# Two graph layers on one core: last norms shared with GpSimd, and weight, score and norm places of layer 1's u stages moved

## The chip, the cores and the metric

The kernel runs on 1 core of one Trainium2 chip. A core has five engines that run their own instruction streams side by side: PE (TensorE, matrix products into PSUM), DVE (VectorE), ACT (ScalarE), POOL (GpSimd) and SP (SyncE, which here only issues DMAs). The metric is device microseconds (us) of one execution; less is better.

## The reference, cut to what matters

For each of two layers, with `N` = 2048 nodes, a batch of 8 and 64 features:

```python
x_g = jnp.einsum('knm,bmc->bnkc', supports, x)        # each node gathers over the graph
w   = jnp.einsum('nd,dkio->nkio', embedding, weight)  # a weight matrix for each node
out = jnp.einsum('bnki,nkio->bno', x_g, w) + bias
x   = _layernorm(x + out, axis=-1)                    # over the 64 features
```

Layer 0 has the supports I, A and 2A²−I. Layer 1 has these and one more, the row softmax of relu(E Eᵀ), where E are the node embeddings (2048 x 16). `_layernorm` subtracts the mean over the 64 features and divides by the square root of the variance plus 1e-5.

## The kernel before, in words

The work is 40 stages of about 30 to 45 us each, five phases of eight blocks of 256 nodes: A0 and B0 are layer 0, A1, Z1 and V1 are layer 1. Stage n is block n % 8 of phase n // 8.

- **A1** (stages 16 to 23, the "u stages" of layer 1) makes u = A x for a block. Stage 16 is a plain product (`straight`, line 484). The others use seven half-size products instead of eight (`strassen`, line 504), with sums of operands that DVE makes ahead.
- **Z1** (stages 24 to 31) makes the softmax support times x. Stage 24 is plain. Stage 25 is called "narrow": its numerators are made by halves, during stage 24.
- **V1** (stages 32 to 39) makes A u. Stage 39 is the last one, and what follows it is the tail.

Each stage has a second job, for the block of the stage before: PE makes the per-node weights (`weights`, line 336: embedding times weight pool, into PSUM tiles `pw`), ACT and DVE copy them to SBUF (`w<-pw`: of three tiles in a job ACT takes the first and the third and DVE the second), PE multiplies them with the features (`apply`, line 370, PSUM tile `po`), and DVE adds what belongs to each node into `acc` under a mask (four instructions of 128x256 for each `apply`). For the last phase of a layer, `post` (line 399) normalizes `acc` in three parts: part 0 makes the mean, subtracts it and has ACT square the result; part 1 sums the squares and has ACT take the root; part 2 makes the reciprocal, multiplies and stores. For layer 1 in the tail the store goes to SP's queue.

The order of instructions on an engine is program order, and it is written by hand. `put(n, place, f)` plans f into stage n. A generator, `product`, issues the stage's matmuls and counts them; whenever the count reaches a place, the planned calls are issued between two matmuls. A stage is 64 counts long if its product is plain and 56 otherwise, and a place is scaled by length/64, so that place 16 in a 56-count stage means "after 14". Every engine takes its instructions in this order, so a call that waits on an engine holds up all that stands behind it there.

Three shared resources matter. Three PSUM tiles (`big`) go around between weights, scores, transposes, bias and `apply`; two further banks hold the accumulators of the products. The weight pools come in four chunks of 8 pairs for a block (512 KB each) through three buffers `wst`; when a job has used up a chunk, its buffer is refilled by a DMA from SP's queue. The jobs of a u stage cover the pairs 0-6, 6-12, 12-18, 18-24, 24-28 and 28-32, so the second job frees chunk 0's buffer, and chunk 3, which that buffer receives, is first used by the fifth job.

For the softmax, `scores_of_rows` (line 733) makes the scores of 128 rows in two halves (PE tile `pr`; DVE applies the relu and takes the row's maximum), and `statistics` (line 745) has ACT make two exponentials of 128x1024 with their sums. `numerators` and `normalize` (line 722, two DVE multiplications of 128x1024 per call in the narrow stage) make the softmax itself.

Of the kernel before, what the change touches and what calls it, by code (L numbers as in the profile page):

```python
# [15 lines left out]
P = 128  # L16
# [32 lines left out]
def two_graph_layers(ctx: ExitStack, tc: tile.TileContext, x, x_t, adj_b, adj_q, layers, out):  # L49
# [231 lines left out]
    class Stage:  # L281
# [114 lines left out]
                    dve.scalar_tensor_tensor(acc, src, mask[:, i:i + 1], acc, op0=ALU.mult, op1=ALU.add)  # L396


        def post(self, part, s0=0, s1=GROUPS):
            a = self.acc[:, s0:s1, :]  # L400
            flat = a.rearrange("p s o -> p (s o)")
            g = s1 - s0
            if self.kk == 0:
                if part == 0:
                    pool.dma_start(out=pd[self.li, self.j], in_=flat)
                return
            if part == 0:
                mean = small.tile([P, GROUPS], F32, tag="mean", name="mean")[:, 0:g]
                dve.tensor_reduce(mean, a, AX.X, ALU.add)
                dve.tensor_scalar(mean, mean, 1.0 / C, None, op0=ALU.mult)  # L410
                dve.tensor_tensor(a, a, mean[:, :, None].to_broadcast([P, g, C]), op=ALU.subtract)
                if self.sq is None:
                    self.sq = one.tile([P, GROUPS, C], F32, tag="sq", name="sq")
                act.activation(self.sq[:, s0:s1, :].rearrange("p s o -> p (s o)"), flat, AF.Square)
            elif part == 1:
                dev = small.tile([P, GROUPS], F32, tag="dev", name="dev")[:, 0:g]
                dve.tensor_reduce(dev, self.sq[:, s0:s1, :], AX.X, ALU.add)
                act.activation(dev, dev, AF.Sqrt, bias=eps, scale=1.0 / C)
                self.dev[s0] = dev
            else:  # L420
                rstd = small.tile([P, GROUPS], F32, tag="rstd", name="rstd")[:, 0:g]
                dve.reciprocal(rstd, self.dev[s0])
                dve.tensor_tensor(a, a, rstd[:, :, None].to_broadcast([P, g, C]), op=ALU.mult)
                if self.li == 1:
                    rows = slice(self.j * NB * B + s0 * P, self.j * NB * B + s1 * P)
                    (pool if s1 - s0 == GROUPS else sp).dma_start(out=rows_of(out[rows, :]), in_=a)
                    return
                pool.dma_start(out=rows_of(x1d[self.j][s0 * P:s1 * P, :]), in_=a)
# [55 lines left out]
        def straight(self, right):  # L484
            accs = [self.accumulator("pu") for _ in range(SB)]
            for m0 in range(0, NJ, 4):
                self.a = adj.next().rearrange("p (m n) -> p m n", n=NB)
                pairs = [(s, m) for s in range(SB) for m in range(m0, m0 + 4)]
                if self.n == 0 and m0 < NJ - 4:
                    pairs.sort(key=lambda at: at[1])  # L490
                for s, m in pairs:
                    pe.matmul(accs[s], self.a[:, m - m0, s * P:(s + 1) * P], right[m],
                              start=(m == 0), stop=(m == NJ - 1))
                    yield 2
                    if m == NJ - 1:
                        copy(s if self.n else 1, self.slabs[s], accs[s])
            self.store_u()

        def store_u(self):
# [4 lines left out]
        def strassen(self, right):  # L504
# [45 lines left out]
            def add(dst, a, b, op=ALU.add):  # L550

                if not isinstance(dst, tuple):
                    dve.tensor_tensor(dst, a, b, op=op)
                elif self.kk == 0:
                    dve.tensor_tensor(self.slabs[dst[0]][:, dst[1] * half:(dst[1] + 1) * half], a, b, op=op)
                else:
                    if self.wide:
                        to = self.pair[dst[0]].features()[64:128, :, :]
                    else:
                        r = 64 if self.narrow else 0  # L560
                        to = self.features()[r:r + 64, dst[0] * P:(dst[0] + 1) * P, :]
                    for par in range(2):
                        of = lambda x: x[64 * par:64 * par + 64, :].rearrange("p (q n) -> p n q", n=nodes)
                        dve.tensor_tensor(to[:, :, 4 * dst[1] + par:4 * dst[1] + par + 3:2], of(a), of(b), op=op)

            c00, c01, c10, c11 = (0, 0), (0, 1), (1, 0), (1, 1)
            w1, w4, v = temps[:3]
# [281 lines left out]
    for n, st in enumerate(stages):  # L849
# [11 lines left out]
        if phase == "A0":  # L861
            for c in range(NJ // 4 if st.j == 1 else 0):
                put(n, 16 * c + 10, st.sums_of_a, c)
            if sevens:
                place_weights(n + 1, (1, 5, 14, 23, 32))
                turned, bursts, posts = 34.5, (39.5, 39.5, 39.5, 39.5), (51,)
            else:
                spread(n + 1, 1, 31, weights)
                turned, bursts, posts = 33, (38, 38, 38, 38), (50,)
        elif phase == "B0":  # L870
            for c in range(NJ // 4 if st.j == 0 else 0):
                put(n, (10, 26, 36, 57)[c], st.sums_of_a, c)
            if st.j == 7:
                spread(n, 35, 54, weights)
                bursts, posts = (0, 0, 6, 10), ()
                put(n + 1, 16, st.load_x, range(SB))
                for k in range(6):
                    put(n + 1, (11 if k < 3 else 12.5) + 0.5 * k, st.post, k % 3, 8 - k // 3 * 8, 16 - k // 3 * 8)
            else:
                spread(n + 1, 3, 13, weights)  # L880
                bursts, posts = (19, 19, 29, 29), (38, 46.5, 50)
                put(n + 2, 5, st.load_x, range(SB))
        elif phase == "A1":
            if sevens:
                place_weights(n + 1, (1, 12.5, 17, 22.3, 31.3))
            else:
                spread(n + 1, 12, 34.5, weights)
            turned, bursts, posts = 4, (43, 43, 43, 43), (56,)
            for s, h, place in ((0, 0, 38), (0, 1, 40), (1, 0, 57), (1, 1, 60)):
                put(*((n, place) if st.j or s == 0 else (n + 1, place - 43)), st.scores_of_rows, s, h)  # L890
            put(n, 41, st.statistics, 0)
            put(*((n, 62) if st.j else (n + 1, 19)), st.statistics, 1)
            put(n + 1, 24, st.store_c)
        elif phase == "V1":
            if st.j:
                put(n, 4, *weights.pop(0))
            spread(n, (22 if 0 < st.j < 7 else 12 if st.j else 4), (62 if st.j < 7 else 42), weights)
            bursts, posts = (4, 4, 4, 4), (15, 19, 23)
            put(n, 20, st.load_z)
# [18 lines left out]
        elif st.narrow:  # L918
            put(24, 1, st.take_halves)
            put(23, 48, st.load_e)  # L920
            for t, places in enumerate(((3, 7, 22), (37, 39.5, 57))):
                for i, place in enumerate(places):
                    put(24, place, *((st.numerators, t, i) if i < 2 else (st.normalize, t)))
            put(26, 10, load_last_phase)
        elif st.wide:
            first, even, odd = (n - 2, (16, 24, 32), (40, 48, 56)) if n % 2 == 0 else (n - 2, (28, 36, 44), (4, 12, 20))
            load = ((25, 40) if n == 28 else (n - 3, 4)) if n % 2 == 0 else (n - 3, 10)
            if n == 26:
                first, even, odd, load = 25, (4, 12, 18), (22, 30, 36), (24, 40)
            elif n == 27:  # L930
                first, even, odd, load = 25, (66, 69, 72), (44, 52, 58), (25, 8)
            put(*load, st.load_e)
            for t, places in enumerate((even, odd)):
                for i, place in enumerate(places):
                    at = (first, place) if place < 64 else (first + 1, place - 64)
                    put(*at, *((st.numerators, t, i) if i < 2 else (st.normalize, t)))
        else:
            st.p = [None] * 8
            for c in range(8):
                if c < 3:  # L940
                    put(n - 1, (50, 54, 62)[c], st.scores, c)
                else:
                    put(n, 8 * (c - 2), st.scores, c)

    last = stages[-1]
    for c in (2, 3):
        put(len(stages) - 1, 50, last.apply, c)
    put(len(stages) - 1, 58, last.post, 0, 8, 16)
    for n, st in enumerate(stages):
        done = 0  # L950
        todo = sorted(plans[n])
# [10 lines left out]
        done = 1000  # L962
        catch_up()
    last.post(1, 8, 16)
    last.post(2, 8, 16)
    last.apply(0)
    last.post(0, 0, 4)
    last.apply(1)
    for part, g0, g1 in ((0, 4, 8), (1, 0, 4), (2, 0, 4), (1, 4, 8), (2, 4, 8)):
        last.post(part, g0, g1)  # L970


# [44 lines left out]
```

## Time and profile before

| | |
|---|---|
| median of 3 runs | 1467.26 us (1466.7 to 1468.25) |
| the profiled execution's own time | 1467.24 us |
| its span, first to last instruction | 1465.5 us |
| PE busy | 1438.7 us, 98% of the span |
| DVE busy | 972.9 us, 66% |
| ACT busy | 485.4 us, 33% |
| POOL busy | 204.5 us, 14%, of which most is issuing DMAs |
| chain that ended last | PE 92%, DVE 3%, DMA 3%, issue 1%, ACT 1% |

The span leaves out 1.7 us of the execution's own time. "PE" is the matmuls and "PEld" the weight loads that overlap them. In a timeline the columns are start, duration, engine, line and operation, output and inputs with shapes, how many were merged, and in brackets the idle time before and who ended it. All instructions carry line 43, that of a helper, so they are told apart by their tiles. Matmul ends are modelled, and each fp32 matmul of the program shows as two records.

### The profile page before, as it was taken

To read this page: it belongs to the slowest core of one execution; us is meant where nothing else is said; L and a number is where in the kernel's file an instruction comes from. 1 tells how busy PE (TensorE), PEld (TensorE's weight loads), DVE (VectorE), ACT (ScalarE), POOL (GpSimd) and SP (SyncE) were. 2 spreads that over 40 slices of the span, in tenths; PEclk is the share of its full clock that TensorE was granted. 3 is DMA by queue.
4 is the path that set the end of the run, shared out by engine and by line. 5 is a ranking of instruction groups with operands and counts; after the bars stand their busy time and mean duration, and the time that the engine had idled before them with its cause. 6 is when DMAs were issued, how large, how long until landed. Compare 5 with 4: busy or idle time off the path is not lost.

```text
span 1465.5 us, 31573 instructions
## 1 busy us (share of the span) xinstructions
PE 1438.7 (98%) x13502; PEld 1185.3 (81%) x13502; DVE 972.9 (66%) x1648; ACT 485.4 (33%) x640; POOL 204.5 (14%) x339
## 2 busy tenths in 40 slices
PE   9999999999999999999999999999999999999996
PEld 4577777778999998577777777799888988888885
DVE  3866666648766666865566666689794566666666
ACT  1444444432212113255444444612110233333232
POOL 5212222110111111211011111011000000000000
PEclk9999999999999999999999999999999999999999
DMA  9888888885666666478787877323314766666662
GB/s 363 279 260 273 293 289 276 277 307 187 197 206 202 204 202 210 150 171 204 183 207 164 199 212 177 43 79 95 83 47 115 248 182 198 193 187 195 191 190 58
DMA packets 88379, 285.50 MB, mean 195 GB/s; under 512 B 14000, under 2 KB 19632, under 8 KB 86640
## 3 DMA queue, kind: packets, MB, share of 16 engines
q1 hardware_dynamic: 55568, 175.13, 40.6%
q0 software_dynamic: 27200, 94.71, 21.9%
q10 hardware_dynamic: 5472, 13.63, 2.8%
q8 instruction: 107, 1.75, 0.5%
q14 instruction: 32, 0.26, 0.1%
HBM read 217.33 MB, written 62.41 MB: 191 GB/s over the span
## 4 chain that ended last, share of the span: by engine, by line
PE 92%; DVE 3%; DMA 3%; issue 1%; ACT 1%; ACTq 0%; DVEq 0%
PE pa L43 67%; PE po L43 14%; PE pw L43 8%; DMA wst<-wd 2%; PE pt L43 1%; PE ps L43 1%; PE pr L43 1%; DMA x<-in_x 1%; DVE acc L43 1%; DVE u L43 1%; DVE mean L43 0%; ACT w L43 0%; DVE w L43 0%; DVE t L43 0%; DVE dev L43 0%
## 5 line engine op out<-in xcount | busy, mean ns | idle before, releaser
L43 ACT ACTIVATE w<-pw 128x1024 f32<-128x1024 f32 x309 | 304.6, 1029 | 403.7 <-PE pw L43 402.5
L43 DVE SCALAR_TENSOR_TENSOR acc<-po,mask,acc 128x256 f32<-128x256 f32 (+1 forms) x640 | 247.0, 426 | 67.3 <-PE po L43 54.5
L43 DVE COPY w<-pw 128x1024 f32<-128x1024 f32 x127 | 155.4, 1224 | 199.6 <-PE pw L43 199.3
L43 PE MATMUL pa<-a,u 128*128 128x128 f32 (+1 forms) x2048 | 264.1, 285 | 2.8 <-issue 2.8
L43 PEld LDWEIGHTS pa<-a,u 128*128 128x128 f32 x2048 | 245.0, 192 | 15.4 <-issue 5.4
L43 PE MATMUL pa<-x,a 128*128 128x256 f32 (+1 forms) x816 | 239.3, 435 | 0.8 <-DMA x<-in_x 0.5
L43 PE MATMUL po<-w,t 128*32 128x256 f32 (+1 forms) x5120 | 206.2, 337 | 5.9 <-issue 4.8
L43 PE MATMUL pa<-u,a 128*128 128x256 f32 x832 | 202.7, 387 | 0.0
L43 PEld LDWEIGHTS pa<-x,a 128*128 128x128 f32 x816 | 149.6, 190 | 61.2 <-issue 37.6
L43 PEld LDWEIGHTS po<-w,t 128*32 128x32 f32 (+1 forms) x5120 | 128.6, 108 | 77.4 <-issue 13.2
L43 PEld LDWEIGHTS pa<-u,a 128*128 128x128 f32 x832 | 151.9, 190 | 28.9 <-issue 5.4
L43 PE MATMUL pw<-e,wst 64*128 64x256 f32 x1680 | 144.7, 295 | 4.3 <-ACT w L43 1.7
L43 PEld LDWEIGHTS pw<-e,wst 64*128 64x128 f32 x1680 | 111.9, 184 | 36.2 <-ACT w L43 11.9
L43 PE MATMUL pa<-a,x 128*128 128x128 f32 x768 | 93.0, 277 | 0.0
L43 PEld LDWEIGHTS pa<-a,x 128*128 128x128 f32 x768 | 88.3, 192 | 2.4
L43 PE MATMUL pa<-w,u 128*128 128x256 f32 x384 | 85.8, 379 | 0.0
L43 PE MATMUL pa<-a,w 128*128 128x128 f32 x672 | 81.3, 277 | 0.0
L43 PEld LDWEIGHTS pa<-w,u 128*128 128x128 f32 x384 | 72.0, 190 | 9.3
L43 PEld LDWEIGHTS pa<-a,w 128*128 128x128 f32 x672 | 77.3, 192 | 2.5 <-issue 1.4
L43 ACT ACTIVATE t<-pt 64x512 f32<-64x512 f32 x64 | 40.6, 635 | 76.5 <-DVE t L43 64.2
L43 ACT ACTIVATE sq<-acc 128x1024 f32<-128x1024 f32 (+2 forms) x19 | 17.5, 922 | 145.1 <-DVE acc L43 135.2
L43 POOL DMA_DIRECT2D e<-ed x80 | 42.1, 531 | 167.5 <-PE pw L43 144.8
(127 smaller groups left out, 1306.2 us busy)
## 6 DMA issues: line engine op xcount, KB each, us to landing
wst<-wd SPq DMA_DIRECT2D x108, 512.0 KB, 6.3
a<-in_adj_q SPq DMA_DIRECT2D x90, 512.0 KB, 5.3
a<-sd SPq DMA_DIRECT2D x88, 512.0 KB, 4.4
sd<-a POOLq DMA_DIRECT2D x24, 512.0 KB, 4.5
bx<-bx POOLq DMA_DIRECT2D x32, 256.0 KB, 5.6
acc<-bx POOLq DMA_DIRECT2D x16, 512.0 KB, 6.7
pd<-acc POOLq DMA_DIRECT2D x16, 512.0 KB, 4.6
acc<-pd POOLq DMA_DIRECT2D x16, 512.0 KB, 8.7
```

What stands on the lines that cost most here:

```text
L43: return self._tc.keep_in_program_order(f(*args, **kwargs))
```

## The change

1. **Tail.** `post` gets an argument that names the engine of its two large elementwise operations (subtract the mean, multiply by the reciprocal). In the last stage the groups 8 to 16 and 0 to 4 give both to POOL; the groups 4 to 8 keep them on DVE. The parts are put in another order. The last four DVE additions before the last `apply` calls are cut by halves of nodes (two instructions of 64x256 become four of 64x128), so that the first 64 nodes are complete earlier. The first two `apply` calls of the last stage stand two matmuls earlier.
2. **u stages 18 to 23.** The six weight jobs of the block before stand at other places: after 11, 14, 18, 23, 28 and 32 matmuls instead of 11, 15, 19, 23, 27 and 31. In stages 17 and 24 they stay where they were.
3. **Stage 17.** The second half of the last scores of block 0 stands two matmuls later, and its statistics with it (after the second weight job, before the third, as before).
4. **Stage 16.** The copy of the second half of u from PSUM moves from ACT to DVE, ahead of a DVE sum of 128x2048.
5. **Stage 24.** The first `normalize` of the narrow stage moves from place 22 to 47.5, behind the 16 masked additions; the second from 57 to 51, with no DVE instruction between its old place and its new one.

No transfer is added or taken away, and the order of DMA issues on SP, ACT and POOL stays.

```diff
-        def post(self, part, s0=0, s1=GROUPS):
+        def post(self, part, s0=0, s1=GROUPS, by=dve):
...
-                dve.tensor_tensor(a, a, mean[:, :, None].to_broadcast([P, g, C]), op=ALU.subtract)
+                by.tensor_tensor(a, a, mean[:, :, None].to_broadcast([P, g, C]), op=ALU.subtract)
...
-                dve.tensor_tensor(a, a, rstd[:, :, None].to_broadcast([P, g, C]), op=ALU.mult)
+                by.tensor_tensor(a, a, rstd[:, :, None].to_broadcast([P, g, C]), op=ALU.mult)
...
-                        copy(s if self.n else 1, self.slabs[s], accs[s])
+                        copy(s if self.li == 0 and self.n else 1 - self.li, self.slabs[s], accs[s])
...
-                    for par in range(2):
-                        of = lambda x: x[64 * par:64 * par + 64, :].rearrange("p (q n) -> p n q", n=nodes)
-                        dve.tensor_tensor(to[:, :, 4 * dst[1] + par:4 * dst[1] + par + 3:2], of(a), of(b), op=op)
+                    parts = 2 if self.n == len(stages) - 1 and dst == c01 else 1
+                    for some in range(parts):
+                        at = slice(some * nodes // parts, (some + 1) * nodes // parts)
+                        for par in range(2):
+                            of = lambda x: x[64 * par:64 * par + 64, :].rearrange("p (q n) -> p n q", n=nodes)[:, at, :]
+                            dve.tensor_tensor(to[:, at, 4 * dst[1] + par:4 * dst[1] + par + 3:2], of(a), of(b), op=op)
...
-            if sevens:
-                place_weights(n + 1, (1, 12.5, 17, 22.3, 31.3))
-            else:
-                spread(n + 1, 12, 34.5, weights)
+            place_weights(n + 1, (12, 15.5, 20.5, 25.5, 32, 36) if 0 < st.j < 7 else (12, 16.5, 21, 25.5, 30, 34.5))
...
-            for s, h, place in ((0, 0, 38), (0, 1, 40), (1, 0, 57), (1, 1, 60)):
-                put(*((n, place) if st.j or s == 0 else (n + 1, place - 43)), st.scores_of_rows, s, h)
+            for s, h, place, later in ((0, 0, 38, 0), (0, 1, 40, 0), (1, 0, 57, 14.2), (1, 1, 60, 19)):
+                put(*((n, place) if st.j or s == 0 else (n + 1, later)), st.scores_of_rows, s, h)
...
-            put(*((n, 62) if st.j else (n + 1, 19)), st.statistics, 1)
+            put(*((n, 62) if st.j else (n + 1, 20)), st.statistics, 1)
...
-            for t, places in enumerate(((3, 7, 22), (37, 39.5, 57))):
+            for t, places in enumerate(((3, 7, 47.5), (37, 39.5, 51))):
...
-        put(len(stages) - 1, 50, last.apply, c)
-    put(len(stages) - 1, 58, last.post, 0, 8, 16)
+        put(len(stages) - 1, 49, last.apply, c)
+    put(len(stages) - 1, 58, last.post, 0, 8, 16, pool)
...
     last.post(1, 8, 16)
-    last.post(2, 8, 16)
+    last.post(2, 8, 16, pool)
     last.apply(0)
-    last.post(0, 0, 4)
+    last.post(0, 0, 4, pool)
     last.apply(1)
-    for part, g0, g1 in ((0, 4, 8), (1, 0, 4), (2, 0, 4), (1, 4, 8), (2, 4, 8)):
-        last.post(part, g0, g1)
+    last.post(0, 4, 8)
+    last.post(1, 0, 4)
+    last.post(1, 4, 8)
+    last.post(2, 0, 4, pool)
+    last.post(2, 4, 8)
```

## The prediction

> **What bounds the kernel now.** I read the page's chain first: 92% of what ended last is PE, and PE is 98% busy. So a change is worth only what it takes from PE's idle time, or from the tail, where PE has finished. Next, PE's waits from stage 16 to 24 (us in total, times, longest):
>
> ```profile
> PE pw L43 <- ACT w L43: 1.7, 3, 1.1
> PE pw L43 <- DMA wst<-wd: 1.5, 3, 0.6
> PE pt L43 <- ACT u L43: 1.0, 1, 1.0
> PE pw L43 <- DVE p L43: 1.0, 1, 1.0
> PE pr L43 <- ACT w L43: 0.5, 1, 0.5
> ```
>
> That is 5.7 us in all, and the edits touch all of it but the longest ACT wait (1.1, stage 24). Third, the timeline of two of these places. Stage 18, a chunk's DMA and the job that waits for it:
>
> ```profile
> 675.36 0.32 SPq L43 DMA_DIRECT2D wst<-wd  x1
> ...
> 684.00 0.74 PE L43 MATMUL pw<-e,wst 64*128 64x256 f32 x8 [0.61 <-DMA wst<-wd]
> ```
>
> Stage 24, where two multiplications of `normalize` stand ahead of what frees a PSUM tile:
>
> ```profile
> 934.23 2.35 DVE L43 TENSOR_TENSOR p<-p,c 128x1024 f32<-128x1024 f32 x2
> 935.80 0.73 PE L43 MATMUL pw<-e,wst 64*128 64x256 f32 x8
> 936.77 0.67 DVE L43 SCALAR_TENSOR_TENSOR p<-ps,c 128x512 f32<-128x512 f32 x1
> 937.49 0.51 PE L43 MATMUL pw<-e,wst 64*128 64x256 f32 x4 [0.96 <-DVE p L43]
> ```
>
> Fourth, the tail. From 1450.66 on DVE works nearly without a gap:
>
> ```profile
> 1450.66 0.86 DVE L43 TENSOR_TENSOR t<-pa,temps 64x256 f32<-64x256 f32 x2 [0.85 <-PE pa L43]
> 1451.55 0.69 DVE L43 TENSOR_REDUCE dev<-sq 128x8 f32<-128x512 f32 x1
> 1453.58 2.04 DVE L43 SCALAR_TENSOR_TENSOR acc<-po,mask,acc 128x256 f32<-128x256 f32 x4
> 1456.32 0.42 DVE L43 TENSOR_TENSOR acc<-acc,mean 128x256 f32<-128x256 f32 x1
> 1456.66 2.04 DVE L43 SCALAR_TENSOR_TENSOR acc<-po,mask,acc 128x256 f32<-128x256 f32 x4
> 1460.72 0.42 DVE L43 TENSOR_TENSOR acc<-acc,rstd 128x256 f32<-128x256 f32 x1
> 1461.90 0.18 DVE L43 RECIPROCAL rstd<-dev 128x4 f32<-128x4 f32 x1 [0.42 <-ACT dev L43]
> 1462.11 0.42 DVE L43 TENSOR_TENSOR acc<-acc,rstd 128x256 f32<-128x256 f32 x1
> ```
>
> The last store is issued at 1462.56, and the span ends at 1465.5. Whatever makes DVE's chain shorter ends the kernel sooner, one to one.
>
> **What the Trainium skill says.** "GPSIMD Engine Reference", § 3.1, gives 4497 ns for a two-input fp32 elementwise operation of 2048 elements on GpSimd: 2.2 ns an element. No run here shows one: POOL's computing so far is memsets and a mask. § 2.1 of that page adds that the first call to a freshly loaded routine pays about 6 us; not shown here either. "SBUF — State Buffer", § SBUF: two separate sides: a GpSimd operation and a DVE operation with two SBUF inputs exclude each other for a whole instruction. DVE's masked additions take one input from PSUM, so they should pass freely.
>
> **u stages 18 to 23.** The time from one `po` to the next in the chain is 42.07, 42.01, 41.52, 41.54, 41.38 and 41.76 us. The fifth has no DMA wait; over it the others lose 0.69, 0.63, 0.14, 0.16 and 0.38, in all 2.0, of which 1.48 is listed (0.61, 0.55, 0.32). A matmul of the program takes 0.48 us here (1.92 for 4). The second job comes one matmul sooner, so chunk 0's buffer is free, and SP issues chunk 3's load, 0.48 us sooner (674.88 for 675.36). The fifth job comes one matmul later: without a wait at 683.87 instead of 683.39. Landing before: about 683.95. So 0.96 us of room stand against at most 0.69 of wait. I do not count on an earlier landing: the DMA rate is about 400 GB/s from 679.5 to 685, three loads share it, and the third starts earlier too (third job at 677.17 for 677.65). With the old landing 0.08 stays in stage 18, 0.02 in stage 19. Moved along: each job issues 8 to 12 matmuls, two copies on ACT or one, and one on DVE. The second job's third tile needs ACT's copy that ends at 674.48; PE gets there at 674.95. Behind the sixth job, half a microsecond later, `pr` and `pb` need its tiles 0.2 to 0.4 us after they are free, and DVE's relu comes 0.14 later, against its idle 0.35 before the masked additions. SP's order is the same. Gain: 1.9; bounds 0.4 (new tile waits in each stage) and 2.0.
>
> **Stage 24.** Without the two multiplications (2.35 us) DVE reaches `p<-ps` when `ps` is there, about 935.1, and is done at 935.8, before PE wants the tile at 936.4. A job of 12 takes 0.91, so PE goes on at 936.70 instead of 937.93. Gain: 1.1; bounds 0.8 and 1.2. The multiplications go behind the masked additions, which end at 958.48: four now, 4.70 us to 963.2. The next DVE instruction, `t<-pa`, starts at 963.27 because PE is not ready earlier. The cover is just enough; if it were gone, each 0.1 us late would be 0.1 on PE only if `t<-pa` (1.4 us, to 964.67) ran past 966.9, where stage 25 takes the bank. So nothing.
>
> **Stages 16 and 17.** PE waits 1.01 at 623.81 for ACT's copy, which starts at 623.16 behind other ACT work, after PE's 622.81. On DVE it can start at about 622.95 and takes 0.68 (the other half's row): PE at 623.65, a gain of 0.15. The sum of 2.28 us behind it ends at 625.9; DVE's next copy starts at 628.64. In stage 17 the later scores take away the wait of 0.50, but they start at 633.02 instead of 632.77, so relu, maximum and ACT's two exponentials are 0.25 later, and ACT's copies of the third job, at 637.60 now, come at 637.85. The fourth job waits for these (0.17 and 0.40 now). PE leaves it 0.25 later, whatever it gained before. Sum: a loss of 0.1, between −0.3 and +0.5.
>
> **Tail.** Step by step, with POOL estimated from the page's price and a start: 1.25 us for 512 elements, 0.7 for 256.
> - `apply` two matmuls sooner: its additions end at 1446.9, not 1447.4. POOL's first subtraction 1448.8 to 1450.1, ACT's square to 1450.85. DVE needs it at 1451.8, so 1.0 us to spare.
> - Additions by halves: 0.43 for 256 elements and, from 0.70 for 512, 1.04 ns an element and 0.155 fixed; 0.29 each for 128. Two done at 1451.24, so PE starts at 1451.31 (−0.27) and the additions start at 1453.31. All four end at 1451.82, the reduction at 1452.55, the reciprocal at 1453.1: in time, since the multiplication of 0.69 is POOL's.
> - Additions to 1455.35, mean to 1456.01; POOL subtracts to 1456.8, ACT squares to 1457.3. Second additions to 1458.08 (they saved 0.27 and 0.34), mean, subtraction and square to 1459.67. DVE's two reductions end at 1459.53 and 1460.11, ACT's roots at 1459.97 and 1460.46.
> - POOL multiplies from 1460.4 to 1461.1, and SP stores. DVE's reciprocal ends at 1460.68; its multiplication, with two SBUF inputs, would end at 1461.13 alone, 1461.55 if it waits for POOL's. Before, 1462.53. SP needs 0.37 to 0.39 for an issue, and the last stands behind POOL's store: about 1461.6 against 1462.56.
>
> Gain: 1.0. Bounds: 1.4 with POOL as fast as DVE's 0.42 and no exclusion; a loss where POOL is slow (rival 3).
>
> **Sum.** −1.9 −1.1 +0.1 −1.0 = −3.9. Of the profiled execution's 1467.24 that leaves 1463.3 (span 1461.6); the median, 1467.26, is the same to 0.02.
>
> **Rivals.**
> 1. The tail gives nothing: POOL takes 0.9 us more for each operation, or the store on SP waits. For: the price is from a page, not a trace. Against: DVE's chain is visibly the bound and loses 1.5 us of work. 1464.3, and 1465 at worst.
> 2. Chunk 3 lands as late as its new job, or tiles become the wait: the jobs' gap of 2.35 us is less than the 2.83 now, with ACT's copies taking 1.94. u stages give 0.4: 1464.8. Against: 0.4 us to spare, worked out above; the stage without a DMA wait has no other.
> 3. Slower: POOL's start. If each POOL operation takes e longer than estimated, the first has 1.0 us to spare, the second subtraction 1.9, and the last multiplication none: the tail loses (e−1.0)+(e−1.9)+e. At e = 2.3 it eats the whole 3.9; at 3.3 the kernel is 3.2 slower, 1470.4. A single 6 us at the first operation costs 5: 1468.3. Against: POOL's memset of 128x2048 takes 1.82 in this profile, its mask 0.31.
>
> **How the numbers follow.** A measurement of this kernel tells about 0.2%, 2.9 us, from no change. As worked out: 0.64 (1462.4 to 1464.2, all faster). Rival 1: 0.15, half of it on each side of 1464.3. Rival 2: 0.13, same. Rival 3: 0.05, of which 0.02 is within the bound. Something unseen, slower: 0.03. Faster 0.64 + 0.07 = 0.71; same 0.08 + 0.13 + 0.02 = 0.23; slower 0.06. The range 1462.4 to 1465.2 takes in rivals 1 and 2 nearly whole.
>
> **What would show it.** Right: no `wst` wait of PE in stages 18, 19 and 23, and `po` to `po` at 41.4; no DVE wait near 936; DVE's multiplications, four in a row, ending before `t<-pa`; the last multiplication about 1.0 earlier against PE's last product. Wrong: a `pw` wait on ACT at the second job; ACT's first square of the tail late behind POOL; a POOL operation over 2 us; the fourth job of stage 17 later than 0.3.

## The result and the profile after

The changed kernel takes 1464.73 us (median of 18 runs), the kernel before 1467.11 us (18 runs beside them). One run of the changed kernel, at 5107.69 us, and one of the kernel before in the second set, at 8318.89 us, lie far outside all others and are left out of the ratios, which compare means (here 1464.17 for 1467.58 us). The ratio is 0.9977, with a 95% interval of 0.9968 to 0.9986: 3.4 us of 1467.1, between 2.1 and 4.7. A second set of runs, in the experiments below, gave 0.9972 (0.9965 to 0.9980). Forecast were 1463.3 us (0.9973), with a range of 1462.4 to 1465.2, and faster as the likeliest sign.

The profiled execution of the changed kernel has a span of 1460.9 us for 1465.5. Of PE's waits over the same stages 16 to 24 (us in total, times, longest), the five groups with 5.7 us have become two with 2.1 (a group of 0.2, `po` waiting for ACT's `t`, is in both kernels and left out):

```profile
PE pw L43 <- ACT w L43: 1.8, 3, 0.9
PE pw L43 <- DMA wst<-wd: 0.3, 1, 0.3
```

The timeline of the changed kernel where the copy of u was moved, stage 16 (start, duration, engine, operation, idle before). In the kernel before, PE began these transposes after a wait of 1.01 us for ACT:

```profile
618.34 4.47 PE L43 MATMUL pa<-x,a 128*128 128x512 f32 x14
623.16 0.60 ACT L43 ACTIVATE u<-pa 128x512 f32<-128x512 f32 x1
623.81 1.09 PE L43 MATMUL pt<-ident,u 128*128 128x128 f32 x8 [1.01 <-ACT u L43]
```

In the changed kernel no wait is left:

```profile
620.25 4.47 PE L43 MATMUL pa<-x,a 128*128 128x512 f32 x14
623.64 0.69 DVE L43 COPY u<-pa 128x512 f32<-128x512 f32 x1
624.56 1.04 PE L43 MATMUL pt<-ident,u 128*128 128x128 f32 x8
```

In stage 24 the job of 12 matmuls is in one piece, and the four multiplications end at 960.74, before DVE has anything else to do:

```profile
934.07 0.69 DVE L43 SCALAR_TENSOR_TENSOR p<-ps,c 128x512 f32<-128x512 f32 x1 [0.53 <-PE ps L43]
934.75 0.97 PE L43 MATMUL pw<-e,wst 64*128 64x256 f32 x12
...
956.12 4.62 DVE L43 TENSOR_TENSOR p<-p,c 128x1024 f32<-128x1024 f32 x4
960.99 1.39 DVE L43 TENSOR_TENSOR t<-pa,c 64x512 f32<-64x512 f32 x2 [0.26 <-PE pa L43]
```

And the tail, where POOL now has four operations:

```profile
1445.45 1.04 POOL L43 TENSOR_TENSOR acc<-acc,mean 128x512 f32<-128x512 f32 x1 [16.72 <-DVE mean L43]
1447.16 1.21 DVE L43 TENSOR_TENSOR t<-pa,temps 64x128 f32<-64x128 f32 x4 [1.79 <-PE pa L43]
1447.81 3.66 PE L43 MATMUL po<-w,t 128*32 128x256 f32 x64 [0.69 <-DVE t L43]
1449.74 1.05 POOL L43 TENSOR_TENSOR acc<-acc,rstd 128x512 f32<-128x512 f32 x1 [3.24 <-DVE rstd L43]
1449.81 2.04 DVE L43 SCALAR_TENSOR_TENSOR acc<-po,mask,acc 128x256 f32<-128x256 f32 x4
1452.59 0.61 POOL L43 TENSOR_TENSOR acc<-acc,mean 128x256 f32<-128x256 f32 x1 [1.80 <-DVE mean L43]
1456.70 0.61 POOL L43 TENSOR_TENSOR acc<-acc,rstd 128x256 f32<-128x256 f32 x1 [3.50 <-DVE rstd L43]
1457.18 0.42 DVE L43 TENSOR_TENSOR acc<-acc,rstd 128x256 f32<-128x256 f32 x1
```

Where the 4.6 us between the two profiled executions went, cut at the starts of the `po` matmuls in the chain that ended last, and at the end of PE's last product (the tail is taken from spans of 1465.47 and 1460.88 us; the texts written ahead of the runs have 14.86 and 13.78 for it, from coarser readings):

| stretch | before | changed | difference | forecast |
|---|---|---|---|---|
| start to `po` of stage 15, not edited | 586.82 | 588.73 | +1.91 | 0 |
| stages 16 and 17 | 62.81 | 61.91 | −0.90 | +0.1 |
| stages 18 to 23 | 250.28 | 248.80 | −1.48 | −1.9 |
| stage 24 | 48.74 | 46.94 | −1.80 | −1.1 |
| to the end of PE's last product, nearly all not edited | 501.99 | 500.76 | −1.23 | 0 |
| tail | 14.83 | 13.74 | −1.09 | −1.0 |

The sum came out near the forecast, but two of its four terms did not, and stretches whose instructions were not edited moved by as much as the edits. So the experiments are read stretch by stretch. Each has the edit at one place, and the other places serve as further executions of what they are.

### The profile page after: what moved, and what is told of

Read it like the earlier page. It is cut to its first block, busy times and chain, and to the rows that moved or that the text cites. A ratio compares the mean times of both kernels' runs of the same rounds, so it can differ in the third digit from the quotient of the medians.

```text
span 1460.9 us, 31574 instructions
## 1 busy us (share of the span) xinstructions
PE 1439.2 (99%) x13502; PEld 1186.3 (81%) x13502; DVE 971.6 (67%) x1647; ACT 485.0 (33%) x639; POOL 208.3 (14%) x343
## 4 chain that ended last, share of the span: by engine, by line
PE 92%; DVE 3%; DMA 3%; issue 1%; ACT 1%; POOL 0%; ACTq 0%; SPq 0%; DVEq 0%
PE pa L43 67%; PE po L43 13%; PE pw L43 8%; DVE acc L43 1%; PE pt L43 1%; DMA wst<-wd 1%; PE ps L43 1%; PE pr L43 1%; DMA t<-t 1%; DVE w L43 1%; DMA a<-in_adj_q 0%; ACT w L43 0%; DMA sd<-sums 0%; DVE t L43 0%; PE pi L43 0%
## 5 line engine op out<-in xcount | busy, mean ns | idle before, releaser
L43 DVE TENSOR_TENSOR t<-pa,temps 64x256 f32<-64x256 f32 (+1 forms) x130 | 54.0, 415 | 18.5 <-PE pa L43 16.5
```

The lines of the kernel that those rows point to most:

```text
L43: return self._tc.keep_in_program_order(f(*args, **kwargs))
```

## The experiments

All kernels of this section compute the full reference. Times of the first seven are those of one execution: 1465.26, 1464.97, 1467.88 and 1463.72 us beside 1466.97 for the kernel before, and 1462.80, 1465.68 and 1462.06 beside 1466.67. They differ by as much as an execution does and decide nothing; the stretches do.

**Stage 24 alone.** The kernel before with

```diff
-            for t, places in enumerate(((3, 7, 22), (37, 39.5, 57))):
+            for t, places in enumerate(((3, 7, 47.5), (37, 39.5, 51))):
```

> Only the two normalize calls of stage 24 are moved (22 to 47.5 and 57 to 51). Read from one apply to the next over stage 24 (first po of stage 23 to first po of stage 24): 48.74 us before, 46.94 in the changed kernel. Theory A, the whole 1.8 us comes from these multiplications: 46.9, with the ACT wait at the second weight job at about 0.5 us. Theory B, the multiplications give 1.1 and the rest is how that ACT wait happens to fall in one execution: about 47.6, with that wait back at 1.1. All other stretches as before.

The stretch took 47.64 us, as theory B has it. The job of 12 is in one piece, and the wait at the second job is back, at 1.24 us (timeline of this kernel):

```profile
930.12 0.74 PE L43 MATMUL pw<-e,wst 64*128 64x256 f32 x8 [1.24 <-ACT w L43]
...
936.19 0.95 PE L43 MATMUL pw<-e,wst 64*128 64x256 f32 x12
```

So the multiplications give 1.1 us, and the other 0.7 of the profiled pair is not theirs. That wait lasted 0.50 to 1.47 us over the eleven profiled kernels, whatever was edited. With it taken off, the stretch is 47.55 to 47.67 us in the four kernels without this edit and 46.33 to 46.44 in the seven with it: a gain of 1.2, clear of all spread. Why the wait itself varies is not shown.

**Stage 16 alone.** The kernel before with

```diff
-                        copy(s if self.n else 1, self.slabs[s], accs[s])
+                        copy(s if self.li == 0 and self.n else 1 - self.li, self.slabs[s], accs[s])
```

> Only the copy of the second half of u in stage 16 goes to DVE. From the transposes of x to those of u in stage 16: 6.35 us before, 5.18 in the changed kernel. Theory A, the matmuls ended about 1.1 us earlier than their modelled end and the copy was late on ACT: 5.2. Theory B, the prediction's 0.15 us: 6.2. From the transposes of u to the first po of stage 17: 25.8 as before, since the scores stay where they were.

Measured: 5.18 us, theory A's number, and 25.77 in stage 17. The timeline of this kernel shows how:

```profile
621.86 0.69 DVE L43 COPY u<-pa 128x512 f32<-128x512 f32 x1
622.78 1.04 PE L43 MATMUL pt<-ident,u 128*128 128x128 f32 x8
```

Theory A has the number, but its reason falls: no result is read ahead of its record's end. The row of 14 merges two shapes that serve two products. The groups of the kernel before between 617 and 624 us, with shapes kept apart (busy us and mean ns of one | idle), and its timeline from 621.1 to 622.9:

```profile
L43 PE MATMUL pa<-x,a 128*128 128x512 f32 x8 | 3.8, 593 | 0.0
L43 PE MATMUL pa<-x,a 128*128 128x256 f32 x8 | 1.9, 379 | 0.0
```

```profile
620.91 1.89 PE L43 MATMUL pa<-x,a 128*128 128x256 f32 x8
```

Of the 14, only the first six, of 128x512, compute the half of u that is copied. They are over when the eight of 128x256 have begun, at about 621.1 in the kernel before. Those eight are already stage 17's first product, and PE waits only after them, from 622.80. ACT, with its table load, two exponentials and the copies of t ahead, took u at 623.16, 2 us after it was there. DVE takes it as soon as its own two copies of t are done:

```profile
620.45 1.38 DVE L43 COPY t<-pt 64x512 f32<-64x512 f32 x2
```

These end at 621.83 and the copy of u at 622.55, before PE is through with the eight. So the whole wait goes. The other kernels repeat it: the two stages took 62.81 to 62.85 us in the four without the edit, 61.61 or 61.62 in three with it alone, and 61.89 to 61.91 in three that also have the later scores of stage 17. The fourth of these, the changed kernel without POOL in the tail, took 63.57; there the granted clock was at half for 3.4 us from 638.9 on, which would account for 1.7.

**Which job of the u stages counts.** The kernel before with only the second job moved, or only the fifth and sixth:

```diff
-                spread(n + 1, 12, 34.5, weights)
+                place_weights(n + 1, (12, 15.5, 21, 25.5, 30, 34.5) if 0 < st.j < 7 else ...)   # second_early
+                place_weights(n + 1, (12, 16.5, 21, 25.5, 32, 36) if 0 < st.j < 7 else ...)     # fifth_late
```

> Of the weight jobs of stages 18 to 23 only the second is moved, one matmul sooner, so the load of chunk 3 is issued 0.48 us sooner and used where it was. The six times from po to po were 42.07, 42.01, 41.52, 41.54, 41.38 and 41.76 us; over 41.36 each this is 2.1 us of excess. Theory A, a load lands so much earlier as it is issued: excess about 0.4. Theory B, the landing is set by the three loads that share the rate and does not come earlier: excess 1.8 to 2.4.

> Of the weight jobs of stages 18 to 23 only the fifth and sixth are moved, one matmul later; the load of chunk 3 is issued where it was. Both theories: 0.48 us off each DMA wait, so excess over 41.36 each of about 0.4 us in all (0.2 in stages 18 and 19, none elsewhere), if the landing stays. If moving the second job was what counted, excess stays above 1.5.

The excess over 6 x 41.36 us, by kernel (a stage in which PE waits for no load takes 41.34 to 41.39 us):

| weight jobs of stages 18 to 23 | excess, us |
|---|---|
| as before (before, norm_late, u_copy) | 2.12, 2.06, 2.76 |
| only the second sooner | 1.93 |
| only the fifth and sixth later | 0.39 |
| the change (after, all_dve, together, after_again) | 0.64, 0.53, 0.04, 0.12 |
| the change, fifth one matmul later still (job24, best) | 0.15, 0.15 |

Theory B holds for the second job. Its load is issued sooner, and the wait is still there, here in stage 23 (timeline of the kernel with the second job moved):

```profile
884.21 0.32 SPq L43 DMA_DIRECT2D wst<-wd  x1
...
893.70 0.51 PE L43 MATMUL pw<-e,wst 64*128 64x256 f32 x4 [1.05 <-DMA wst<-wd]
```

One load tells little, since its landing differs between executions (by 1.8 us in stage 19 with the load at its old place). Counted from the `po` at which the stages are cut, the load of chunk 3 landed after 33.66 us on average where the load was issued at the old place (21 landings in four kernels), after 33.73 here (5), and after 33.50 in the kernels with the whole change (35 landings in six kernels), although the last two issue it 0.43 us sooner. So little or nothing of the earlier issue reaches the landing. That the three loads share the rate is the likely reason; no run here isolates it.

Moving the fifth and sixth jobs alone takes away 1.7 of 2.1 us. What it leaves is 0.21 us in stage 18 and 0.11 in stage 23. Its 0.39 lies within what the whole change leaves, so that the second job's move adds anything is not shown; the third job's, one matmul sooner, was not tried alone.

**POOL's part in the tail.** The changed kernel with `pool` taken out of the four calls of `post`:

```diff
-    last.post(2, 8, 16, pool)
+    last.post(2, 8, 16)
     last.apply(0)
-    last.post(0, 0, 4, pool)
+    last.post(0, 0, 4)
...
-    last.post(2, 0, 4, pool)
+    last.post(2, 0, 4)
```

> The changed kernel with nothing on POOL in the tail: the new order of the parts and the additions by halves stay, DVE makes all multiplications and subtractions. Read from the end of PE's last product to the end of the span: 14.86 us before, 13.78 in the changed kernel. Theory A, POOL's share is what shortens DVE's chain: 0.69 and about 0.3 us come back, so 14.7 to 14.8. Theory B, the new order and the halves give most of it: about 14.1.

Measured: 14.51 us, between the two. DVE's chain behaves as theory A has it: its last multiplication ends 11.51 us after PE's last product, for 10.47 in the changed kernel, 1.04 more. But only 0.77 of that reaches the end. The last two multiplications end 0.55 us apart here and 0.29 in the changed kernel, while their stores land 0.55 and 0.54 apart (the latter read from the changed kernel's second profile): in the changed kernel the last store has to wait for the one ahead. Of the tail's 1.1 us, order, halves and the earlier `apply` calls give 0.32 without POOL, and POOL on top of them 0.77. The first three were not taken apart.

**Do POOL and DVE exclude each other.** The changed kernel with one root and one reciprocal for eight groups:

```diff
-    last.post(1, 0, 4)
-    last.post(1, 4, 8)
-    last.post(2, 0, 4, pool)
-    last.post(2, 4, 8)
+    (both sums into one tile, one root, one reciprocal of 128x8, then)
+    for s0, by in ((0, pool), (4, dve)):
+        by.tensor_tensor(a, a, rstd[:, s0:s0 + 4, None].to_broadcast([P, 4, C]), op=ALU.mult)
```

> The changed kernel with one root and one reciprocal for the last eight groups, so that POOL's last multiplication (groups 0 to 4) and DVE's (groups 4 to 8), which both read two SBUF operands, are released at the same moment. If they exclude each other for a whole instruction, as the SBUF page of the Trainium skill has it, one of them ends 0.4 to 0.6 us late: the later end comes at least 1.0 us after the common start, and one of the two shows a late start or about double its 0.42 or 0.61 us. If they don't, DVE takes 0.42 and POOL 0.61 us from about the same start.

```profile
1459.45 0.42 DVE L43 TENSOR_TENSOR acc<-acc,rstd 128x256 f32<-128x256 f32 x1
1459.50 0.85 POOL L43 TENSOR_TENSOR acc<-acc,rstd 128x256 f32<-128x256 f32 x1 [3.99 <-DVE rstd L43]
```

DVE takes its usual 0.42, POOL 0.85 for 0.61. The later end is 0.90 us after the first start, less than the 1.0 that was set for a full exclusion and more than the 0.66 without any. In this one execution POOL's operation was 0.24 us longer, and DVE's was not. What "SBUF — State Buffer" of the Trainium skill says in § SBUF: two separate sides, that the later one blocks until the other is through, fits if POOL's first 0.13 us need no access; that is reckoned (0.85 less the 0.37 to DVE's end leaves 0.48 of 0.61), not shown. The other way round the block does not appear: in all four profiled kernels with the changed tail, DVE's multiplication begins 0.13 us before POOL's ends and keeps its 0.42.

**Three more places.** The changed kernel with the scores of stage 17 back, the fifth job at 29 and the second job of stage 24 one matmul later:

```diff
-    ... (1, 0, 57, 14.2), (1, 1, 60, 19) ... (n + 1, 20), st.statistics
+    ... (1, 0, 57, 14), (1, 1, 60, 17) ... (n + 1, 19), st.statistics
-    place_weights(n + 1, (12, 15.5, 20.5, 25.5, 32, 36) if 0 < st.j < 7 else (12, 16.5, 21, ...))
+    place_weights(n + 1, (12, 15.5, 20.5, 25.5, 33, 36) if 0 < st.j < 7 else (12, 16.5 + st.j // 7, 21, ...))
```

> The changed kernel with three more places: the late scores of stage 17 back where they were before, the fifth weight job of stages 18 to 23 one matmul later still (29), the second weight job of stage 24 one matmul later. Stage 17, from the transposes of u to the first po: 25.8 us (26.1 in the changed kernel) if the scores' move costs what was worked out. The six times from po to po: all within 0.15 of 41.36, if the room of a further 0.48 us covers the landing. Stage 24: 46.5 us if PE's wait of 0.5 to 1.5 us at the second job comes from being too early by less than one matmul; 46.9 or more if it is set by a copy that moves along with it.

Stage 17 took 25.78 us: the move of the scores costs 0.3. All six u stages are at 41.37 to 41.39. Stage 24 took 47.29 us: its wait is 0.86 us, within the 0.50 to 1.47 of the old place, so a matmul of 0.48 us does not remove it. Whether it takes something off, one execution can't tell:

```profile
927.62 1.09 PE L43 MATMUL pw<-e,wst 64*128 64x256 f32 x12 [0.86 <-DVE w L43]
```

**A better version, timed beside the changed kernel.** The first two of these places, without that of stage 24, and the last store but one on ACT's queue:

```diff
-                    (pool if s1 - s0 == GROUPS else sp).dma_start(out=rows_of(out[rows, :]), in_=a)
+                    (pool if s1 - s0 == GROUPS else act if s0 == 0 else sp).dma_start(out=rows_of(out[rows, :]), in_=a)
```

> The changed kernel once more, timed beside the next one. Expected ratio to before 0.9975 to 0.9978 (the recorded one is 0.9977); at the places that the edits touch the same times as before: 5.2 us between the transposes in stage 16, 26.1 in stage 17, DMA excess below 0.7 us over the six u stages, stage 24 at 46.4 us plus its ACT or DVE wait, tail 13.8 us.

> The changed kernel with the late scores of stage 17 where they were before (25.8 us for 26.1), the fifth weight job of stages 18 to 23 one matmul later still (DMA excess 0 to 0.2 us for 0.6), and the store of the groups 0 to 4 issued from ACT's queue, so that the last store does not stand behind it on SP (tail 13.5 us for 13.8). In all 0.8 to 1.2 us less than the changed kernel in the profile; by time a ratio to before of 0.9968 to 0.9972, which may not stand apart from the changed kernel's.

The changed kernel: 1463.07 us (18 runs), ratio 0.9972 (0.9965 to 0.9980). At the edited places 5.18, 26.08, an excess of 0.12, stage 24 at 47.31 with a wait of 0.88, tail 13.74. The better version: 1461.51 us (5 runs), ratio 0.9965 (0.9952 to 0.9979), beside 1467.34 for the kernel before. It is faster than the kernel before; that it beats the changed kernel the intervals don't show. By its profile (span 1459.4 for 1461.0) stage 17 gave back 0.3, and the excess was as small in both; 0.9 of the 1.6 lie in the start, which is not edited. The store gave nothing: the tail took 13.80 us. It is issued at once now,

```profile
1455.70 0.42 DVE L43 TENSOR_TENSOR acc<-acc,rstd 128x256 f32<-128x256 f32 x1
1455.86 0.41 ACTq L43 DMA_DIRECT2D out<-acc  x1
1456.15 0.39 SPq L43 DMA_DIRECT2D out<-acc  x1
```

and lands no sooner, because the two stores' data go one behind the other. The DMA engines' rates in this kernel, in 40 slices of 0.125 us from 1455 to 1460:

```profile
GB/s 0 0 0 0 0 0 0 0 0 0 0 0 0 0 43 172 258 246 211 209 213 223 217 215 90 0 0 0 0 0 0 0 0 0 0 0 0 0 0 0
```

One block of 1.3 us for twice 128 KB, at about 215 GB/s, in packets under 512 bytes. In the changed kernel the same view shows one block of the same length, so its data too already went without a gap.

## Why the prediction was right, and where it was wrong

**The whole.** Sign, time and range were right: forecast −3.9 us, measured −3.4 (−4.7 to −2.1), then −4.1. This is partly luck: the edited stretches gave over 1 us more than forecast, and the times gave less than the edited stretches. So each term is taken by itself.

**u stages, −1.9: right.** Excess 2.1 to 2.8 without the edit, 0.04 to 0.64 with it: a gain of about 2.0. The step that did not count on an earlier landing was right as well: the fifth job's 0.48 us did the work, and the second job's earlier load came hardly earlier. What the prediction missed is that the wait wanders. With the same places the longest one was 0.61 us in stage 18, 1.17 in stage 21 and 0.64 in stage 23 in three kernels, so the room of 0.96 against "at most 0.69" was less comfortable than it looked. Rival 2 fell: no tile became the wait.

**Stage 24, −1.1: right.** Measured alone, 1.1, and 1.2 over all profiles with the other wait taken off. The profiled pair showed 1.8 because that wait, which the prediction left where it was, happened to be 0.6 shorter. The four multiplications were hidden, with 0.26 us to spare for the 0.07 worked out.

**Stages 16 and 17, +0.1: wrong, measured −0.9.** The step that failed is "after PE's 622.81". That time was read from a timeline row of 14 matmuls, as the end of u's product. It is the end of the next product's first half, which PE does while u waits; u was there at about 621.1. ACT was thus 2 us late, and the wait of 1.01 us was what PE had not filled with other matmuls. With the copy on DVE it goes as a whole: 1.17 us of the stretch instead of 0.15. The other half was right: the scores' move costs 0.3 us, and undoing it gives them back. The chain is the one that was named: counted from the second weight job, ACT's copies of the third start 0.32 us later (638.62 with the job at 631.85, for 637.60 with 631.15), behind relu, maximum and two exponentials.

**Tail, −1.0: right, 1.09.** The last multiplication came 10.47 us after PE's last product, 10.49 by the working. POOL took 1.04 and 0.61 us for the estimated 1.25 and 0.7, from the price in "GPSIMD Engine Reference", § 3.1 (2.2 ns an element; 2.0 and 2.4 here). Its first operation was not slow, so rival 3 fell, and the 6 us of § 2.1 did not appear here. Rival 1 fell too, since the end came 0.77 us sooner through POOL. Two steps were wrong. The last store is not late because of SP's issue, but because its data wait for those of the store ahead. And DVE's chain does not shorten the kernel one to one: of the 1.04 us that POOL took from it, 0.77 arrived.

**What stays open.** The edited stretches give 5.3 us in the profiled pair, and about 5 from all profiles; the times give 3.4 to 4.1. The start, to the `po` of stage 15, has the same instructions in all kernels. It took 586.28 to 588.45 us in the five with the tail of before (mean 587.1), and 586.60 to 589.10 in the six with the new tail (mean 588.2). Most of this is there early: the DVE sum `sums<-a` that starts at 67.45 us in the kernel before starts on average at 67.45 in the five and 68.22 in the six. That would be the difference, but the ranges overlap, and no run here was made to tell chance from a cause. The −1.23 us between stage 24 and the last product do not belong to the change: the other four kernels with the tail of before took 500.73 to 500.76 us there, as the changed kernel did.

## What to carry to other kernels

Add a change up stretch by stretch, and compare the stretches too: a total near the forecast can hide two wrong terms, and unedited stretches move by one or two microseconds. Where a wait for a transfer differs from execution to execution, using the data later can be worth more than asking for it sooner, as it was here, where three loads were under way together. And a merged row of the timeline can hold two shapes with two purposes: split it by shape before its end is used as the time at which an input is ready, since a wait shows only that part of a lateness which other work does not fill.

## What the hardware showed that was not expected

- A two-input POOL operation of 128x256 took 0.61 us alone and 0.85 when a DVE multiplication of the same size started with it; DVE's kept 0.42. POOL's 128x512 beside DVE's additions, which read one of their inputs from PSUM, took 1.04 to 1.05 us, and the four additions 2.04, as without POOL.
- Loads of 512 KB issued 0.43 us sooner landed 0.16 us sooner on average (33.66 us after the `po` at which the stages are cut, at the old place, 33.50 in the kernels with the whole change), and not at all where only the second job was moved (33.73).
- Two stores of 128 KB, issued 0.29 us apart from SP's and ACT's queues, landed 0.55 us apart, as two that SP issued 0.48 apart did (0.54).
